# Second biases of a mixture-of-experts layer added through the gates, in attention's output product

## The chip, the core and the metric

The kernel runs on one core of a Trainium2 chip. Its engines work side by side and each takes its instructions in order: TensorE (PE, with weight loads shown apart as PEld), VectorE (DVE), ScalarE (ACT), GpSimd (POOL), and SyncE (SP), which here issues most of the DMAs. The metric is the device time of one execution in microseconds. The profile shows one execution on the same core.

## The reference, cut to what matters

Two layers are computed over `x` of shape (8, 512, 128), in float32. Each layer normalizes `x`, and adds an attention and a mixture of experts of the normalized rows to it. The change concerns layer 1:

```python
xn = layernorm(x)
x = x + attention1(xn) + experts1(xn)

# experts1, for each token t of the 4096
probs = softmax(xn @ gate_w.T)              # 8 experts
topk_probs, topk_idx = top_k(probs, 2)
hidden  = relu(xn @ w1[e] + b1[e])          # 128 -> 512
all_out = hidden @ w2[e] + b2[e]            # 512 -> 128
y = sum over the two experts e of topk_probs * all_out[e]

# attention1: the last product of each batch row
out = (gl * local + gr * remote) @ w_out
```

The second bias of an expert is a row of 128 numbers. What a token gets of all of them is the sum over its two experts of gate times `b2[e]`, which is also the product of the token's row of eight gates (six of them zero) with the 8x128 matrix `b2`.

## The kernel before, in words

**Order.** The kernel doesn't issue its instructions as it is written. A `Recorder` keeps every operation of every stage, with its engine, the tiles it reads and writes, and an estimated duration, and then a list scheduler writes out one order for all five engines (`order`). Each operation has a rank, which is spread evenly over the interval that the table `PLAN` gives to its stage: "layer0", "attention1" and "output" have an interval for each of the eight batch rows, "route" and "experts1" one for each of three groups. Among the operations that can start, the one with the earliest estimated start goes first, then the lower rank; none may run more than 60 units of rank ahead of the oldest that is left. Buffers of a tag in SBUF are given out in the order of rank, and an operation that opens a PSUM tile also claims the SBUF tiles that the later users of it open. Since all recorded instructions are issued from one helper line, the profile puts them under L389, and they are told apart by the names of their tiles. The scatters are at L1371, the loads of the experts' weights at L1336 and L1340, and the loads of the second bias at L1344.

**Fill products.** Where the estimate leaves PE idle for at least 0.6 units ahead of a fresh PSUM bank, `_fill` (L362) puts products of a tile of bfloat16 zeros there. Their results are thrown away.

**Layer 0** (`layer0`, eight times) ends with the new `x1`, the normalized rows in DRAM (`x_rows`), their transpose `x2p`, and the logits of layer 1's router. Inside it the experts' gates go through a transpose and an ACT copy (`gate_rows`: PSUM tile `gp`, SBUF tile `gT` of 8x512), are stored to DRAM and come back as broadcasts `gbc`.

**Routing** (`route`, for groups of 2, 3 and 3 batch rows). Two one-hot tiles `pick` hold the token's first and second expert, `gw` the two gates. Prefix sums over PE products give every pair of token and expert a place in a list ordered by expert, in tiles of 128 places, each tile of one expert. The outcome is `row_i` and `token_i`, the rows to scatter to and to gather from, and `own_i`, each tile's expert. There are 23, 31 and 31 tiles, 85 in all.

**Experts** (`experts1`). For a tile: SP reads the expert's number and loads its `w1` and `w2` (256 KB each) and its second bias, one row of 128 broadcast to 128 partitions (64 KB). POOL gathers the tokens' rows. PE transposes them and makes four products into `hp`; ACT adds the first bias and takes relu (four instructions, `ht`); PE makes four accumulated products into `yp`. Then DVE adds the second bias while it moves the tile out of PSUM (`ys`), and POOL scatters `ys` to `y_rows`:

```python
ys = work.tile([P, C], F32, tag="ys", name=f"ys{nm}_{j - 1}", bufs=YS)
nc.vector.tensor_add(ys, yp[:, :C], b2)
scatter(j - 1, ys)
```

**Attention** (`attention1`, eight times) computes a remote and a local part. The remote part is in `aT`. The local part ends with products into the PSUM tile `pv`; DVE forms `loc` from it, POOL adds `loc` to `aT`, PE makes four products of `aT` with `wo1` into the bank `fp`, and DVE adds `fp` to `x1`. `aT` and `loc` have one buffer each.

**Output** (`output`, eight times) loads the two rows per token from `y_rows`, and DVE adds gate times row to `x1` in eight instructions; then `x1` is stored.

Of the kernel before, what the change touches and what calls it, by code (L numbers as in the profile page):

```python
# [10 lines left out]
F32 = mybir.dt.float32  # L11
# [3 lines left out]
ALU = mybir.AluOpType  # L15
# [4 lines left out]
P = 128  # L20
B, N, C = 8, 512, 128
H, D = 16, 8
NT = N // P
E = 8
# [10 lines left out]
GROUP_OF = [(h, i) for h, n in enumerate(GROUPS) for i in range(n)]  # L35
# [400 lines left out]
def two_layers_kernel(  # L436
# [14 lines left out]
    nc = Recorder(tc.nc)  # L451
# [18 lines left out]
    def load(dst, src, queue=nc.sync):  # L470

        queue.dma_start(dst, src)
        landing[0] += 4e-6 * int(np.prod(list(dst.shape))) / 0.25
        nc.ops[-1].delay = max(2.0, landing[0] - 0.5 * len(nc.ops))
# [30 lines left out]
    we_sb = const.tile([P, E, C], F32, name="we_sb")  # L505
    load(we_sb, expert_w, nc.scalar)

    ro_sb = const.tile([P, C], F32, name="ro_sb")
    for half in (slice(0, LC), slice(LC, P)):
        load(ro_sb[half], r_out_w)  # L510
# [71 lines left out]
    def mm(o, lhsT, rhs, start=True, stop=True):  # L582
        nc.tensor.matmul(o, lhsT, rhs, start=start, stop=stop)

    def bank(name, parts=P):
        t = ps.tile([parts, 512], F32, tag="bank", name=name)
        nc.banks[t[:].tensor.name] = t[:]
        return t
# [106 lines left out]
    def gate_rows(g, name, tile):  # L695

        gp = bank(f"gp{name}")
        for t in range(NT):
            nc.tensor.transpose(gp[:E, t * P : (t + 1) * P], g[:, t, :], ident)
        gT = tile(keep, [E, N], "gT", f"gT{name}")  # L700
        nc.scalar.copy(gT, gp[:E])
        return gT
# [11 lines left out]
    for h, n in enumerate(GROUPS):  # L714
# [1 line left out]
        rows = 2 * max(GROUPS) * N + _tiles(n) * P  # L716
        y_rows.append(tc.nc.dram_tensor(f"y_rows_{h}", [rows, C], F32, kind="Internal").ap())
        logits.append(keep.tile([P, n * NT, E], F32, tag=f"logits{h}", name=f"logits_{h}", bufs=1))
    places = {}


    OTHER = {
# [200 lines left out]
    def attention1(b):  # L923

        nm = f"_{b}"
# [214 lines left out]
        nc.vector.scalar_tensor_tensor(loc, gsb[:, 0, :], 1.0, pv, ALU.add, ALU.mult)  # L1140
        nc.gpsimd.tensor_tensor(aT, aT, loc, ALU.add)
        yield
        fp = bank("fp" + nm)
        for t in range(NT):
            ts = slice(t * P, (t + 1) * P)
            mm(fp[:, ts], aT[:, ts], wo1)
        xf = x1.rearrange("p t c -> p (t c)")
        nc.vector.tensor_add(xf, xf, fp)
        late[b] = x1
# [2 lines left out]
    def route(h):  # L1152


        nm = f"_{h}"
# [14 lines left out]
        nc.vector.tensor_tensor(gw[:, 1], mx2, mx, ALU.subtract)  # L1170
        nc.scalar.activation(gw[:, 1], gw[:, 1], AF.Exp, bias=zero)
        nc.vector.tensor_mul(gw[:, 1], gw[:, 1], rs)
        m = small.tile([P, GT, E], F32, tag="ex16", name="m" + nm, bufs=1)
        nc.vector.tensor_add(m, pick[:, 0], pick[:, 1])
        mf = m.rearrange("p t e -> p (t e)")
# [133 lines left out]
    def experts1(h):  # L1309

        nm = f"_{h}"
        TILES = _tiles(GROUPS[h])
        row_i, token_i, _, bias, own_i = places[h]
        ws, xgs, xts, hts, numbers = {}, {}, {}, {}, {}

        def fetch(j):

            if j % QUAD == 0:
                n = min(QUAD, TILES - j)
                number = own_i[0:1, j : j + n]  # L1320

                def load(q=j // QUAD):
                    _, numbers[q] = tc.nc.values_load_multi_w_load_instructions(
                        number, engines=(mybir.EngineType.SP,), min_val=0, max_val=E - 1,
                        skip_runtime_bounds_check_because="a count of experts, held under E on the chip",
                    )

                nc.add("SP", load, [], [number], 1.5, 0.0)
                fetch.last = nc.ops[-1]
            first = work.tile([P, FF], F32, tag="w1", name=f"w1{nm}_{j}", bufs=3)  # L1330
            second = work.tile([P, NFC, C], F32, tag="w2", name=f"w2{nm}_{j}", bufs=4)
            third = work.tile([P, C], F32, tag="b2", name=f"b2{nm}_{j}", bufs=4)

            def load_first():
                e = bass.ds(numbers[j // QUAD][j % QUAD], 1)
                tc.nc.sync.dma_start(first, w1[e].rearrange("e p f -> (e p) f"))  # L1336

            def load_second():
                e = bass.ds(numbers[j // QUAD][j % QUAD], 1)
                tc.nc.sync.dma_start(second, w2[e].rearrange("e (k p) c -> p (e k) c", p=P))  # L1340

            def load_third():
                e = bass.ds(numbers[j // QUAD][j % QUAD], 1)
                tc.nc.sync.dma_start(third, experts_b[e, 1].to_broadcast([P, C]))  # L1344

            for move, to in ((load_first, first), (load_second, second), (load_third, third)):
                nc.add("SP", move, [to], [], 0.55, 3.3)
                nc.ops[-1].follows = (fetch.last,)
            ws[j] = first, second, third

        def gather(q):
            js = range(q * QUAD, min((q + 1) * QUAD, TILES))
            if not len(js):
                return
            xg = work.tile([P, QUAD, C], F32, tag="xgt", name=f"xgt{nm}_{q}", bufs=2)
            for a, j in enumerate(js):
                nc.gpsimd.indirect_dma_start(
                    xg[:, a], None, x_rows[h],
                    bass.IndirectOffsetOnAxis(ap=token_i[:, j : j + 1], axis=0),
                )  # L1360
            xgs[q] = xg

        views = dram_disjoint_views(y_rows[h], TILES)
        scattered[h] = []

        def scatter(j, ys):

            ids = row_i[:, j : j + 1]

            def store():  # L1370
                tc.nc.gpsimd.indirect_dma_start(  # L1371
                    views[j], bass.IndirectOffsetOnAxis(ap=ids, axis=0), ys, None
                )

            nc.add("POOL", store, [], [ys, ids], 1.25, 2.4)
            scattered[h].append(nc.ops[-1])

        def turn(q):
            if q not in xgs:
                return  # L1380
            xg = xgs.pop(q)
            n = min(QUAD, TILES - q * QUAD)
            tp = bank(f"tpx{nm}_{q}")
            for a in range(n):
                nc.tensor.transpose(tp[:, a * P : (a + 1) * P], xg[:, a], ident)
            xt = work.tile([P, QUAD * P], F32, tag="xt", name=f"xt{nm}_{q}", bufs=2)
            nc.scalar.copy(xt[:, : n * P], tp[:, : n * P])
            xts[q] = xt

        for j in range(AHEAD):  # L1390
            fetch(j)
        gather(0)
        yield
        turn(0)
        gather(1)
        yield
        for j in range(TILES + 1):
            if j < TILES:
                if j + AHEAD < TILES:
                    fetch(j + AHEAD)  # L1400
                q, a = divmod(j, QUAD)
                if a == 1:
                    turn(q + 1)
                    gather(q + 2)
                hp = bank(f"hp{nm}_{j}")
                for k in range(NFC):
                    mm(
                        hp[:, k * P : (k + 1) * P], ws[j][0][:, k * P : (k + 1) * P],
                        xts[q][:, a * P : (a + 1) * P],
                    )  # L1410
                ht = work.tile([P, NFC, P], F32, tag="ht", name=f"ht{nm}_{j}", bufs=2)
                for k in range(NFC):
                    nc.scalar.activation(
                        ht[:, k], hp[:, k * P : (k + 1) * P], AF.Relu, bias=bias[:, k, j : j + 1]
                    )
                hts[j] = ht
                yield
            if j:
                ht, (_, w2k, b2) = hts.pop(j - 1), ws.pop(j - 1)
                yp = bank(f"yp{nm}_{j - 1}")  # L1420
                for k in range(NFC):
                    mm(
                        yp[:, :C], ht[:, k], w2k[:, k],
                        start=k == 0, stop=k == NFC - 1,
                    )
                ys = work.tile([P, C], F32, tag="ys", name=f"ys{nm}_{j - 1}", bufs=YS)
                nc.vector.tensor_add(ys, yp[:, :C], b2)
                scatter(j - 1, ys)
                yield

# [21 lines left out]
    def load_next(b):  # L1452
        xs[b] = load_x(b)
        if b == 1:
# [6 lines left out]
    PLAN = {  # L1461
        "load": ((0, 1), (46, 47), (92, 93), (138, 139), (184, 185), (230, 231), (276, 277)),
        "layer0": (
            (0, 1), (0, 10), (1, 39), (77, 134),
            (121, 154), (178, 309), (241, 418), (313, 760),
        ),
        "route": ((68, 100), (273, 384), (789, 901)),
        "attention1": (
            (33, 150), (148, 194), (204, 270), (284, 611),
            (549, 789), (924, 1084), (1023, 1271), (1198, 1498),  # L1470
        ),
        "experts1": ((68, 410), (427, 1006), (967, 1293)),
        "output": (
            (676, 701), (627, 663), (1181, 1203), (995, 1107),
            (1262, 1379), (1408, 1425), (1456, 1524), (2493, 2506),
        ),
    }

# [77 lines left out]
```

## Time and profile before

| | |
|---|---|
| runs, median (lowest to highest) | 643.65 us (640.91 to 647.41), 3 runs |
| the profiled execution's own time | 641.0 us |
| its span, first to last instruction | 639.1 us |
| mean granted PE clock, as a share of full speed | 0.947 |
| busy: PE, PEld | 563.8 us (88%), 465.2 us (73%) |
| busy: DVE, ACT, POOL | 476.3 us (75%), 343.9 us (54%), 402.7 us (63%) |
| DMA | 91.63 MB, mean 143 GB/s |

The busy time of an engine is the time in which at least one of its instructions ran. A group's row gives the instructions that share engine, operation and tile names: count, busy time, mean duration in ns, then the idle time of the engine just before them and who ended it. A product of float32 operands shows as two instructions, and products overlap, so the busy time of a group of products is less than count times mean. The chain of waits is followed back from the last instruction: at each step to what released it, or to the instruction ahead of it on its engine.

### The profile page before, as it was taken

To read this page: it belongs to the slowest core of one execution; us is meant where nothing else is said; L and a number is where in the kernel's file an instruction comes from. 1 tells how busy PE (TensorE), PEld (TensorE's weight loads), DVE (VectorE), ACT (ScalarE), POOL (GpSimd) and SP (SyncE) were. 2 spreads that over 40 slices of the span, in tenths; PEclk is the share of its full clock that TensorE was granted. 3 is DMA by queue.
4 is the path that set the end of the run, shared out by engine and by line. 5 is a ranking of instruction groups with operands and counts; after the bars stand their busy time and mean duration, and the time that the engine had idled before them with its cause. 6 is when DMAs were issued, how large, how long until landed. Compare 5 with 4: busy or idle time off the path is not lost.

```text
span 639.1 us, 15660 instructions
## 1 busy us (share of the span) xinstructions
PE 563.8 (88%) x5487; PEld 465.2 (73%) x5487; DVE 476.3 (75%) x1297; ACT 343.9 (54%) x950; POOL 402.7 (63%) x422
## 2 busy tenths in 40 slices
PE   9989888798899898789999799888798988999894
PEld 3478576487777687678978679878586777888852
DVE  2797899979898899997768777878437552856594
ACT  3624639354947754475774474543744347457620
POOL 3045143788678559647668768867668586787562
PEclk8999999899999999999979899798989799899986
DMA  4044135264434246247545665677457485687222
GB/s 153 19 145 137 66 102 147 53 187 123 126 98 120 64 158 148 58 140 213 150 129 164 185 188 179 155 216 211 156 179 196 129 237 141 171 238 245 60 83 67
DMA packets 106532, 91.63 MB, mean 143 GB/s; under 512 B 8940, under 2 KB 84086, under 8 KB 106454
## 3 DMA queue, kind: packets, MB, share of 16 engines
q1 hardware_dynamic: 100582, 78.41, 42.1%
q0 software_dynamic: 5440, 11.15, 6.3%
q10 hardware_dynamic: 432, 1.07, 0.5%
q8 instruction: 44, 0.72, 0.5%
q14 instruction: 34, 0.28, 0.1%
HBM read 80.70 MB, written 9.90 MB: 142 GB/s over the span
## 4 chain that ended last, share of the span: by engine, by line
PE 37%; DVE 28%; POOL 12%; issue 9%; ACT 6%; DMA 6%; SPq 0%; POOLq 0%; DVEq 0%; ACTq 0%
PE yp L389 7%; PE hp L389 6%; PE sc L389 4%; DMA gbc<-gd 3%; POOL m L389 3%; PE rp L389 3%; DVE pw L389 3%; PE pv L389 3%; DVE xg L389 2%; POOL pw L389 2%; POOL xgt L389 2%; POOL y_rows L1371 2%; DVE m L389 2%; POOL xg L389 2%; DVE x L389 2%
## 5 line engine op out<-in xcount | busy, mean ns | idle before, releaser
L389 ACT ACTIVATE ht<-hp,bias 128x128 f32<-128x128 f32 x340 | 101.4, 373 | 51.2 <-PE hp L389 34.1
L1371 POOL DMA_INDIRECT y_rows<-ys,row_i x85 | 88.1, 1036 | 48.4 <-issue 9.8
L389 POOL DMA_INDIRECT xgt<-x_rows,token_i x85 | 87.4, 1029 | 24.8 <-issue 18.6
L389 PE MATMUL yp<-w,ht 128*128 128x128 f32 x680 | 94.6, 286 | 1.9 <-issue 1.6
L389 PEld LDWEIGHTS hp<-xt,w 128*128 128x128 f32 x680 | 86.6, 198 | 12.7 <-issue 6.7
L389 PE MATMUL hp<-xt,w 128*128 128x128 f32 x680 | 94.4, 285 | 1.2 <-DVE ys L389 0.7
L389 PEld LDWEIGHTS yp<-w,ht 128*128 128x128 f32 x680 | 86.9, 199 | 7.3 <-issue 5.3
L389 PE MATMUL rp<-we_sb,xg 128*128 128x128 f32 x512 | 67.9, 281 | 6.3 <-POOL xg L389 4.7
L389 PEld LDWEIGHTS rp<-we_sb,xg 128*128 128x128 f32 x512 | 62.2, 194 | 11.9 <-POOL xg L389 7.4
L389 POOL TENSOR_TENSOR xg<-xT,gbc 128x512 f32<-128x512 f32 x32 | 42.8, 1338 | 37.3 <-DMA gbc<-gd 25.9
L389 PE MATMUL pv<-pw,vb 128*32 128x64 f32 (+1 forms) x1088 | 37.9, 226 | 15.6 <-POOL pw L389 11.5
L389 PE MATMUL sc<-kT,qe 32*128 32x64 f32 x1024 | 45.7, 296 | 6.1 <-issue 4.8
L389 PEld LDWEIGHTS pv<-pw,vb 128*32 128x32 f32 x1088 | 33.7, 117 | 23.5 <-POOL pw L389 16.5
L389 PEld LDWEIGHTS sc<-kT,qe 32*128 32x128 f32 x1024 | 40.2, 205 | 11.9 <-issue 7.5
L389 POOL TENSOR_TENSOR pw<-pt,csb 128x512 f32<-128x512 f32 x32 | 42.5, 1328 | 3.5 <-DVE pt L389 3.3
L389 POOL TENSOR_TENSOR m<-m,amx 128x512 f32<-128x512 f32 x32 | 33.8, 1065 | 14.7 <-DVE amx L389 12.8
L389 POOL TENSOR_TENSOR m<-m,ard 128x512 f32<-128x512 f32 x32 | 34.4, 1076 | 12.7 <-DVE ard L389 3.4
L389 DVE TENSOR_TENSOR ys<-yp,b 128x128 f32<-128x128 f32 x85 | 23.5, 278 | 23.6 <-PE yp L389 19.5
L389 DVE TENSOR_TENSOR pw<-pt,csb 128x512 f32<-128x512 f32 x32 | 40.6, 1268 | 0.3
L389 POOL TENSOR_TENSOR le<-le,lrd 128x128 f32<-128x128 f32 (+3 forms) x32 | 24.0, 756 | 25.3 <-DVE lrd L389 18.3
L389 DVE COPY_PREDICATED m<-csb,sc 128x256 f32<-128x256 int32 x64 | 25.3, 435 | 19.5 <-issue 7.9
L389 ACT ACTIVATE m<-m,zero_b 128x512 f32<-128x512 f32 x32 | 23.2, 724 | 29.6 <-POOL m L389 29.6
(261 smaller groups left out, 1232.6 us busy)
## 6 DMA issues: line engine op xcount, KB each, us to landing
w<-in_w_dram SPq DMA_DIRECT2D x170, 256.0 KB
gbc<-gd SPq DMA_DIRECT2D x64, 256.0 KB
b<-in_experts_b_dram SPq DMA_DIRECT2D x85, 64.0 KB
yg<-y_rows SPq DMA_DIRECT2D x16, 256.0 KB
x<-in_x_dram SPq DMA_DIRECT2D x8, 256.0 KB
x_rows<-xn SPq DMA_DIRECT2D x8, 256.0 KB
out_dram<-x SPq DMA_DIRECT2D x8, 256.0 KB
xgt<-x_rows,token_i POOLq DMA_INDIRECT x85
```

The lines of the kernel that those rows point to most:

```text
L389: r.ENGINES[name], lambda: call(*args, **kwargs), aps[:1], aps[1:], time, delay, shape
L1371: tc.nc.gpsimd.indirect_dma_start(views[j], bass.IndirectOffsetOnAxis(ap=ids, axis=0), ys, None)
```

## The change

The second bias leaves the tiles of the experts. `route` forms `gates`, for each token its gate at its two experts and zero elsewhere. At the end of `attention1` these are transposed to `gT` (8x512, in the buffer of `loc`), and four products of `gT` with the 8x128 tile `b2_sb`, loaded once, open the accumulation in `fp`, ahead of the four old products. In `experts1` the load of the second bias goes, and ACT copies the tile out of PSUM in place of DVE's addition. The table `PLAN` has other numbers throughout.

```diff
+    b2_sb = const.tile([E, C], F32, name="b2_sb")
+    load(b2_sb, experts_b[:, 1])
...
     # attention1, after aT += loc
+        h, hb = GROUP_OF[b]
+        gT = gate_rows(gates1[h][:, hb * NT : (hb + 1) * NT], "1" + nm, lambda pool, sh, tag, name: (
+            work.tile(sh, F32, tag="loc", name=name, bufs=1)
+        ))
         fp = bank("fp" + nm)
-        for t in range(NT):
-            ts = slice(t * P, (t + 1) * P)
-            mm(fp[:, ts], aT[:, ts], wo1)
+        tiles = [slice(t * P, (t + 1) * P) for t in range(NT)]
+        for ts in tiles:
+            mm(fp[:, ts], gT[:, ts], b2_sb, start=ts.start == 0, stop=False)
+        for ts in tiles:
+            mm(fp[:, ts], aT[:, ts], wo1, start=False, stop=ts.stop == N)
...
     # route, after gw
+        both = small.tile(sh, F32, tag="rpw", name="gated" + nm, bufs=1)
+        nc.vector.tensor_tensor(both, pick, gw.unsqueeze(3).to_broadcast(sh), ALU.mult)
+        gates = small.tile([P, GT, E], F32, tag="gates", name="gates" + nm)
+        nc.vector.tensor_add(gates, both[:, 0], both[:, 1])
+        gates1[h] = gates
...
     # experts1
-            third = work.tile([P, C], F32, tag="b2", name=f"b2{nm}_{j}", bufs=4)
...
-            def load_third():
-                e = bass.ds(numbers[j // QUAD][j % QUAD], 1)
-                tc.nc.sync.dma_start(third, experts_b[e, 1].to_broadcast([P, C]))
-
-            for move, to in ((load_first, first), (load_second, second), (load_third, third)):
+            for move, to in ((load_first, first), (load_second, second)):
...
-                nc.vector.tensor_add(ys, yp[:, :C], b2)
+                nc.scalar.copy(ys, yp[:, :C])
...
     PLAN = {
         "layer0": (
-            (0, 1), (0, 10), (1, 39), (77, 134),
-            (121, 154), (178, 309), (241, 418), (313, 760),
+            (0, 1), (0, 6), (3, 45), (41, 184),
+            (132, 227), (197, 282), (255, 454), (390, 826),
         ),
-        "route": ((68, 100), (273, 384), (789, 901)),
+        "route": ((26, 48), (228, 322), (801, 988)),
         "attention1": (
-            (33, 150), (148, 194), (204, 270), (284, 611),
-            (549, 789), (924, 1084), (1023, 1271), (1198, 1498),
+            (40, 86), (110, 159), (187, 257), (319, 696),
+            (596, 1011), (987, 1227), (1232, 1332), (1290, 1606),
         ),
-        "experts1": ((68, 410), (427, 1006), (967, 1293)),
+        "experts1": ((63, 364), (375, 1040), (1032, 1380)),
...
```

More of the change, by code (lines that the diff above doesn't have):

```diff
@@ L718, in two_layers_kernel @@
         logits.append(keep.tile([P, n * NT, E], F32, tag=f"logits{h}", name=f"logits_{h}", bufs=1))
-    places = {}
+    places, gates1 = {}, {}
     OTHER = {
@@ L1340, in load_second @@
                 tc.nc.sync.dma_start(second, w2[e].rearrange("e (k p) c -> p (e k) c", p=P))
-            def load_third():
-                e = bass.ds(numbers[j // QUAD][j % QUAD], 1)
-                tc.nc.sync.dma_start(third, experts_b[e, 1].to_broadcast([P, C]))
-            for move, to in ((load_first, first), (load_second, second), (load_third, third)):
+            for move, to in ((load_first, first), (load_second, second)):
                 nc.add("SP", move, [to], [], 0.55, 3.3)
                 nc.ops[-1].follows = (fetch.last,)
-            ws[j] = first, second, third
+            ws[j] = first, second
         def gather(q):
@@ L1418, in experts1 @@
             if j:
-                ht, (_, w2k, b2) = hts.pop(j - 1), ws.pop(j - 1)
+                ht, (_, w2k) = hts.pop(j - 1), ws.pop(j - 1)
                 yp = bank(f"yp{nm}_{j - 1}")
@@ L1463, in two_layers_kernel @@
         "layer0": (
-            (0, 1), (0, 10), (1, 39), (77, 134),
-            (121, 154), (178, 309), (241, 418), (313, 760),
+            (0, 1), (0, 6), (3, 45), (41, 184),
+            (132, 227), (197, 282), (255, 454), (390, 826),
         ),
-        "route": ((68, 100), (273, 384), (789, 901)),
+        "route": ((26, 48), (228, 322), (801, 988)),
         "attention1": (
-            (33, 150), (148, 194), (204, 270), (284, 611),
-            (549, 789), (924, 1084), (1023, 1271), (1198, 1498),
+            (40, 86), (110, 159), (187, 257), (319, 696),
+            (596, 1011), (987, 1227), (1232, 1332), (1290, 1606),
         ),
-        "experts1": ((68, 410), (427, 1006), (967, 1293)),
+        "experts1": ((63, 364), (375, 1040), (1032, 1380)),
         "output": (
-            (676, 701), (627, 663), (1181, 1203), (995, 1107),
-            (1262, 1379), (1408, 1425), (1456, 1524), (2493, 2506),
+            (707, 747), (602, 635), (1386, 1421), (1092, 1223),
+            (1290, 1354), (1495, 1551), (1550, 1665), (2587, 2790),
         ),
```

## The prediction

> **What bounds the kernel now.** I read the busy shares of the whole page first.
>
> ```profile
> PE 563.8 (88%) x5487; PEld 465.2 (73%) x5487; DVE 476.3 (75%) x1297; ACT 343.9 (54%) x950; POOL 402.7 (63%) x422
> ```
>
> TensorE leads, but an average over stages hides where. So I cut the span where the DVE writes `row_i` (row 114.4 us, then about 308 and 450, the three ends of `route`) and where the last expert tile is done, and asked for busy time by stage.
>
> ```profile
> 0.00:114.40 114.40, 102.43 (x675) 72.16 (x676) 89.63 (x303) 59.58 (x143) 36.50 (x56) 0.99 0.36 110
> 114.40:308.00 193.60, 172.78 (x1814) 143.59 (x1813) 171.36 (x484) 114.03 (x301) 136.33 (x134) 0.98 0.44 125
> 308.00:450.00 142.00, 127.37 (x1332) 114.71 (x1330) 107.88 (x268) 78.87 (x232) 105.60 (x106) 0.93 0.61 177
> 450.00:608.00 158.00, 140.91 (x1479) 122.81 (x1478) 85.93 (x202) 88.05 (x269) 111.41 (x116) 0.93 0.60 173
> 608.00:639.10 31.10, 20.33 (x202) 11.90 (x199) 21.49 (x47) 3.35 (x7) 12.84 (x11) 0.77 0.27 77
> ```
>
> The columns are the stretch, its length, busy us of PE, PEld, DVE, ACT, POOL, clock, DMA share, GB/s. Call the stages A to D and the tail. In A the kernel is latency bound, and 19 us of PE's busy time in the first 128 us are the fill products on `zeros`. In B PE and DVE are both 89% busy. In C and D PE is 90% and 89% busy, while DVE falls to 76% and 54%. So the additions that this change takes from DVE lie mostly where DVE has slack, and the products it gives to PE lie where PE has little. In the chain of waits PE holds 37%, DVE 28%, POOL 12%, issue 9%, ACT 6%: the limit passes from engine to engine, and PE is the commonest holder.
>
> The tail shows in the chain as a purely serial end:
>
> ```profile
> 626.19 1.93 PE pv L389 x36
> 628.12 3.10 PE fp L362 x7
> 631.22 1.44 PE fp L389 x8
> 632.66 0.02 issue
> 632.68 0.70 DVE x L389
> ```
>
> The seven fill products put ahead of `fp` last longer than the wait that they cover: `aT` is ready at 630.2 us, the first `fp` product runs at 631.0.
>
> **The change, part by part.** The rows used:
>
> ```profile
> L389 DVE TENSOR_TENSOR ys<-yp,b 128x128 f32<-128x128 f32 x85 | 23.5, 278 | 23.6 <-PE yp L389 19.5 <-PE tpx L389 1.4 <-PE hp L389 1.2
> L389 ACT COPY pT<-tpu 128x128 f32<-128x128 f32 x8 | 2.1, 268 | 5.3 <-PE tpu L389 3.0 <-PE hp L389 1.6 <-PE yp L389 0.7
> L389 PE MATMUL fp<-wo,aT 128*128 128x128 f32 x64 | 9.5, 295 | 4.7 <-POOL aT L389 4.7
> L389 PE MATMUL gp<-csb,g 128*8 128x128 f32 x32 | 5.6, 288 | 1.7 <-issue 0.8 <-ACT gsb L389 0.5 <-DVE g L389 0.4
> L389 ACT COPY gT<-gp 8x512 f32<-8x512 f32 x8 | 4.6, 571 | 7.9 <-PE gp L389 7.8 <-issue 0.2
> L389 PE MATMUL lv<-ro_sb,lat 64*128 64x128 f32 x64 | 5.7, 297 | 3.9 <-DVE lat L389 3.6 <-PE sl L389 0.4
> ```
>
> 1. *The eviction moves.* DVE loses 85 additions, 23.5 us: by stage tables of `ys`, 4.0 before 288 us, 19.5 after. ACT gains 85 PSUM copies of 128 columns; the row of that form is `pT`, 268 ns, so 22.8 us, and ACT goes from 344 to 367. The latency to the scatter stays (278 against 268). The copy waits for `yp` in ACT's queue, as the addition did in DVE's (19.5 us). Behind it stand `ht` of the next tile, the `m` and `pT` copies: what PE needs next. ACT already waits 34.1 us on `hp`, so it is usually ahead of PE, and I cost the wait at nothing; if the cover goes, each badly placed copy costs up to the 0.27 us it lasts, some 5 us over the tiles at the outside.
>
> 2. *The gates' products.* Per batch 4 transposes to 8 rows, one ACT copy of 8x512, and 4 products of `b2_sb` ahead of the 4 old ones. Transposes: 32 at 5.6/32, 5.6 us. Copies: 8 x 571 ns, 4.6 us of ACT. For the products no row has 8 rows of contraction. The nearest is `fp` (same bank, same columns): 9.5 us for the 64 recorded instructions. The lower end is `lv`, 64 rows, 5.7 us; but its products alternate between two halves of the rows and overlap, and these all use the same eight. A guess that work shrinks with the rows would give 9.5 x 8/128 = 0.6 us. The Trainium skill (TensorE: Matmul & The Clock Gate, "Why this matters for your kernels") speaks against that: a single product over 32 rows takes as long as one over 128, and only concurrent row groups gain. No run here shows it for 8 rows; I take 9.5. PE gains 15 us, one eighth of it in the tail.
>
> 3. *Does PE have room for 15 us?* The Trainium skill (Trainium Kernel Development and Optimization, "Best Practices") says to judge the distance to the limit by the busy share of the weight loads and not of the products. By that, PE stands at 73%, C and D at 81% and 78%, and the 13 us outside the tail would vanish in gaps. By the products' rows C and D have 10 to 11% idle, most of it in pieces of under 1 us before an instruction of PE's own ("issue"), which other work can't enter; then 13 us of work cost 13 to 14.5. I take the products, nearer to the second, because waits on other engines are a small part of PE's idle time there.
>
> 4. *Route.* Each of three gets a product like `rpw` (346 ns) and a half-size addition: about 0.6 us each, 2 us of DVE, before `m` and so on the way to the first expert tile.
>
> 5. *Loads.* 85 broadcasts of 64 KB go, 5.6 of 91.6 MB, and 85 issues of SP with their waits:
>
> ```profile
> SPq L1340 <- PE yp L389: 62.9, 31, 9.9
> SPq L1336 <- PE hp L389: 45.6, 21, 8.4
> SPq L1344 <- DVE ys L389: 13.4, 13, 3.9
> ```
>
> L1344 is the issue of this load. Behind it in SP's queue stand the next tile's `w1` and `w2` and the gates' broadcasts. But SP mostly waits for PE to free the weights' buffers, and PE waited for weights 0.9 us in all; once, at 559 us, a late weight load is in the chain with 6.2 us. So the gain is 0 to 6 us; I take 1. The one new load, 8 rows at the start, stands behind `experts_row` in SP's queue and costs the next loads one issue, about 0.5 us; they are not on the first chain.
>
> 6. *The order.* All of `PLAN` is new, so the order matters as much as the operations. I weighed each instruction in both orders by its row (PE 0.27 us for a product of 128 columns, 0.15 a transpose; DVE by the means of its forms). Such sums exceed busy time by a tenth, since neighbours overlap; below they are brought down by 0.9. A: DVE +3.5 before `row_i_0`, PE the same. B: PE -9, DVE -21. C: PE +18, DVE +5. D: PE 0. So layer 0's and attention's DVE work leaves the stage where DVE binds and lands where `ys` made room; PE's work goes with it, into the stage where PE is 90% busy. Costs: A +2 (DVE is 78% busy). B between -9 (PE decides) and -21 (DVE decides), both being 89% busy: middle, -15. C +18/0.9 = +20 if PE is full, less some 3 for waits on DVE that go: +17. D -1 for the loads.
>
> 7. *The tail.* `gT` takes the buffer of `loc` (tag `loc`, one buffer), so its copy can start only when POOL has added `loc` into `aT`; the order puts the eighth batch's transposes behind seven fill products, two more fills behind those, then the gates' products, then the old ones. From 631.2 us on: transposes about 0.8 us at the lowered clock (0.60 for the four at 601 us, and 1.44 against 1.06 us for four products), copy with its handing over 0.8, products of the gates as long as the old, 1.44. Together +3 us, all on the path. In the other batches this chain lies beside expert tiles.
>
> Sum: 2 - 15 + 17 - 1 + 3 = +6 on the profiled execution's own 641.0 us (span 639.1), thus 647; the median of the runs shown is 643.65, on which +6 would be 650. I take 649, between the two.
>
> **Rivals.**
> - *PE decides everywhere* (slower). B gains only 9, C pays 20, the tail 3, A 3: +17, and with copies that hold `ht` back in ACT's queue up to +20. For it: PE is the engine with the least room from 308 us on, and PE's total grows by 15. Against: B has DVE as full as PE. Time about 659; it decides if DVE is no longer the limit in B already at -9.
> - *DVE's relief decides* (faster). B gains 21, C loses only 12 because the short waits of PE on POOL and ACT, which wait for DVE, shrink, loads give 4, the tail costs 3, A 2: -8 to -10. Time about 632. For it: DVE and POOL hold 40% of the chain. Against: DVE has 24% and 46% to spare in C and D.
> - *The edits do nothing and the new order alone decides*: this would give either sign, and is held in the two above.
>
> **The numbers.** Forecast (+1 to +12 us) 0.48, PE everywhere 0.26, DVE's relief 0.26. Within 1% (637.2 to 650.1, about what a measurement of this kernel tells from no change) lie some six tenths of the forecast and a little of the second rival: 0.31. Slower 0.43, faster 0.26. The range, from the middle of one rival to the middle of the other with a little of the rest, is 629 to 661; the forecast's own is 642 to 654.
>
> **What would show it.** `ys` copies near 268 ns on ACT; 96 more PE records on `fp` and `gp`, with 8-row products as long as 128-row ones; last `pv` to last `x` in 3 us more; `row_i` of the second route 10 to 20 us earlier, and C 15 to 20 us longer. If C does not lengthen, the faster rival is right; if `row_i` comes no earlier, the slower one.

## The result, and the profile after

The changed kernel takes 660.55 us (median of 4 runs, 659.5 to 663.57), the kernel before 643.68 us on the same chip: the ratio is 1.0266, with a 95% interval of 1.0204 to 1.0328. The profiled execution took 659.5 us, its span 657.7 us. That is 18.5 us more than the 641.0 us of before, against a forecast of 6 for that execution, and 16.9 us between the medians.

The busy shares, from the head of the page of the changed kernel:

```profile
PE 574.9 (87%) x5577; PEld 476.3 (72%) x5577; DVE 473.7 (72%) x1218; ACT 365.5 (56%) x1043; POOL 405.7 (62%) x422
```

PE has 11.1 us more to do, but it also sits idle longer: span less busy time was 639.1 - 563.8 = 75.3 us and is 657.7 - 574.9 = 82.8 us. ACT gains 21.6 us. DVE is only 2.6 us less busy though 23.5 us of additions left it: others of its instructions took longer, most of all the 64 in `output` that add gate times row (26.8 us before):

```profile
L389 DVE SCALAR_TENSOR_TENSOR x<-yg,gw,x 128x128 f32<-128x128 f32 x64 | 31.8, 526 | 5.0 <-DMA yg<-y_rows 4.9
```

POOL is 3 us busier with the same number of instructions.

The groups that were moved or added, from the groups kept apart by shape:

```profile
L389 ACT COPY ys<-yp 128x128 f32<-128x128 f32 x85 | 22.9, 270 | 29.0 <-PE yp L389 21.5 <-remote 3.3 <-PE lv L389 3.0
L389 PE MATMUL fp<-b_sb,gT 8*128 8x128 f32 x64 | 9.1, 281 | 2.2 <-ACT gT L389 1.4 <-ACT ht L389 0.8
L389 PE MATMUL fp<-wo,aT 128*128 128x128 f32 x64 | 9.4, 291 | 0.0
L389 PE MATMUL gp<-csb,gates 128*8 128x128 f32 x32 | 5.3, 291 | 0.0
```

Every new duration is as it was taken: 270 ns for the copy (268 taken), 5.3 us for the transposes (5.6), and 9.1 us for the gates' products (9.5), although they contract over 8 rows. What they add to PE's busy time is less than their sum, since they overlap with neighbours: 11.8 us by the run without them below, not 15. So the surprise is not in what the single instructions cost.

The stages, cut at the ends of the three routes and at the end of the last tile's `ys`, are in the answer of the changed kernel by stretches (stretch, length, busy us of PE, PEld, DVE, ACT, POOL, granted clock, DMA share, GB/s):

```profile
0.00:116.80 116.80, 100.92 (x725) 71.32 (x726) 89.96 (x307) 58.70 (x139) 41.50 (x57) 0.95 0.33 104
116.80:305.00 188.20, 170.07 (x1685) 144.66 (x1684) 164.22 (x419) 113.31 (x308) 123.89 (x124) 0.95 0.41 116
305.00:468.70 163.70, 145.99 (x1494) 129.62 (x1493) 113.69 (x282) 95.52 (x295) 118.80 (x119) 0.96 0.57 166
468.70:620.30 151.60, 133.50 (x1392) 115.08 (x1390) 80.30 (x160) 91.74 (x290) 104.17 (x108) 0.93 0.52 149
620.30:657.70 37.40, 24.46 (x288) 15.62 (x287) 25.49 (x54) 6.25 (x14) 17.36 (x15) 0.87 0.22 66
```

Read the length of each row first. Stage A is 2.4 us longer than before, B 5.4 us shorter (193.6 before), C 21.7 us longer (142.0 before), and from the third route to the end nothing moves (189.1 and 189.0). The loss is one stage, C, with 18.6 us more PE busy time in it than before, and too little given back by B, where PE is busy 2.7 us less and DVE 7.1.

The granted clock has a part in how this divides: it is 0.95 in B (0.98 before) and 0.96 in C (0.93 before). In a later run of the same order, without the gates' products, B had 0.98 and 185.6 us, C 0.93 and 169.0 us. So the two stages are safer read as a sum, 16.3 us more than before.

New waits stand where the change was made. From the changed kernel's list of waits (total us, times, longest):

```profile
POOL y_rows L1382 <- ACT ys L389: 40.9, 28, 6.6
...
DVE x L389 <- PE fp L389: 25.9, 6, 5.8
```

And from that of the kernel before:

```profile
POOL y_rows L1371 <- DVE ys L389: 9.6, 9, 2.1
...
DVE x L389 <- PE fp L389: 5.7, 3, 3.8
```

They are the first suspects: the evictions on ACT, and the longer chain to `fp`.

The last batch row's end, from the chain of waits of the changed kernel (start, length, what):

```profile
643.14 1.92 PE pv L389 x36
645.06 2.92 PE gp L362 x7
647.98 0.45 PE gp L389 x4
...
648.51 0.58 ACT gT L389
649.09 0.04 issue
649.13 2.26 PE fp L389 x16
651.39 0.02 issue
651.41 0.70 DVE x L389
```

The serial chain of gates is there as read from the order: seven fill products, transposes, copy (two more fill products beside it), eight recorded products in front of the old eight. From the end of `pv` to the start of DVE's addition it is 6.4 us, where it was 4.6.

### The profile page after: what moved, and what is told of

Its sections match the earlier page's. It is cut to its first block, busy times and chain, and to the rows that moved or that the text cites. A ratio compares the mean times of both kernels' runs of the same rounds, so it can differ in the third digit from the quotient of the medians.

```text
span 657.7 us, 15523 instructions
## 1 busy us (share of the span) xinstructions
PE 574.9 (87%) x5577; PEld 476.3 (72%) x5577; DVE 473.7 (72%) x1218; ACT 365.5 (56%) x1043; POOL 405.7 (62%) x422
## 4 chain that ended last, share of the span: by engine, by line
PE 37%; DVE 33%; POOL 10%; ACT 8%; issue 7%; DMA 3%; another core or an unknown queue 0%; SPq 0%; POOLq 0%; DVEq 0%; ACTq 0%
PE hp L389 6%; PE yp L389 6%; PE pv L389 3%; DVE x L389 3%; PE rp L389 3%; DVE pw L389 2%; PE fp L389 2%; POOL y_rows L1382 2%; DMA gbc<-gd 2%; ACT ht L389 2%; POOL pw L389 2%; POOL m L389 2%; DVE pt L389 2%; DVE asd L389 2%; POOL xgt L389 2%
## 5 line engine op out<-in xcount | busy, mean ns | idle before, releaser
L1382 POOL DMA_INDIRECT y_rows<-ys,row_i x85 | 91.3, 1074 | 54.1 <-ACT ys L389 40.9
L389 PE MATMUL hp<-xt,w 128*128 128x128 f32 x680 | 96.7, 289 | 5.7 <-ACT xt L389 5.6
L389 POOL DMA_INDIRECT xgt<-x_rows,token_i x85 | 83.8, 986 | 22.2 <-issue 19.4
L389 PEld LDWEIGHTS rp<-we_sb,xg 128*128 128x128 f32 x512 | 62.7, 194 | 17.7 <-issue 5.0
L389 POOL TENSOR_TENSOR pw<-pt,csb 128x512 f32<-128x512 f32 x32 | 45.7, 1429 | 4.0 <-DVE pt L389 2.9
L389 PE MATMUL pv<-pw,vb 128*32 128x64 f32 (+1 forms) x1088 | 38.1, 227 | 11.1 <-POOL pw L389 9.6
L389 PE MATMUL sc<-kT,qe 32*128 32x64 f32 x1024 | 38.9, 278 | 6.9 <-issue 4.5
L389 POOL TENSOR_TENSOR m<-m,amx 128x512 f32<-128x512 f32 x32 | 34.6, 1084 | 14.9 <-DVE amx L389 13.4
L389 PEld LDWEIGHTS sc<-kT,qe 32*128 32x128 f32 x1024 | 35.0, 189 | 12.1 <-issue 7.8
L389 ACT COPY vb<-v 32x128 f32<-32x128 f32 x128 | 37.7, 295 | 6.6 <-PE pv L389 2.8
L389 DVE TENSOR_REDUCE lmx<-sl 128x8 f32<-128x128 f32 (+3 forms) x32 | 14.3, 482 | 35.7 <-PE sl L389 23.2
L389 ACT COPY ys<-yp 128x128 f32<-128x128 f32 x85 | 22.9, 270 | 29.0 <-PE yp L389 21.5
L389 DVE TENSOR_TENSOR pw<-pt,csb 128x512 f32<-128x512 f32 x32 | 36.7, 1148 | 0.6
```

Of the source, the lines that this page charges most:

```text
L389: r.ENGINES[name], lambda: call(*args, **kwargs), aps[:1], aps[1:], time, delay, shape
L1382: tc.nc.gpsimd.indirect_dma_start(views[j], bass.IndirectOffsetOnAxis(ap=ids, axis=0), ys, None)
```

## The experiments

Three theories are told apart. Theory 1: the products that PE was given are the cost, whatever the order. Theory 2: the new table is, since it puts more PE work between the second and the third route. Theory 3, formed after the first four runs: it is the written-out order as a whole, that is how well a table fits the operations it orders, and the single edits are small. Where times from different chips are compared, the ratios to the kernel before are what counts.

**The two tables and the two sets of edits, exchanged.** Edit of the first run: the table `PLAN` of before in the changed kernel. Edit of the second: the changed kernel's table in the kernel before, and nothing else.

```diff
     # e1_edits_old_plan, against the changed kernel
-        "route": ((26, 48), (228, 322), (801, 988)),
+        "route": ((68, 100), (273, 384), (789, 901)),
     # e2_new_plan_alone, against the kernel before
-        "route": ((68, 100), (273, 384), (789, 901)),
+        "route": ((26, 48), (228, 322), (801, 988)),
     # and so for every stage
```

> All edits of the change, with the table PLAN of before. Theory 1 (the products on PE are the cost, the new intervals only deal work out among stages): 652 to 662 us, within 5 us of the changed kernel at 660.5. Theory 2 (the new order is the cost, since it gives PE more work in the stage from the second to the third route): 640 to 650 us. If it is slower than 665, the new intervals were a repair for the edits.

> The kernel before with the changed kernel's PLAN and none of its other edits. Theory 1 (products): 640 to 650 us. Theory 2 (order): 652 us or more, and the stretch between the second and third row_i stays near 160 us, as in the changed kernel (163.6), against 142.1 before.

Measured, with the kernel before at 643.3 us on that chip: 668.7 us for the edits with the old table (ratio 1.0438, 1.0372 to 1.0503), and 671.75 us for the old kernel with the new table (1.0433, 1.0378 to 1.0488). Each table is far worse with the other kernel than with its own: with the old table the edits cost 25 us, with the new one they save 11 us against leaving them out. So neither the edits nor the table has a price by itself; a table belongs to the operations that it was drawn up for. Theory 1 misses both runs, and its claim that the intervals only deal work out falls. Theory 2 has the second run right (652 or more; C even longer than near 160 us) and the first wrong (640 to 650): the old table is no repair of the changed kernel. The first run is past 665, where the expectation says that it is the other way round: the new intervals repair part of what the edits do to the old ones.

The first run loses its time in A and B (123.7 and 208.3 us, against 114.4 and 193.6 before), with C at 141.5. The second run shows where the new table puts work. Its answer by stretches:

```profile
120.60:309.00 188.40, 163.90 (x1636) 138.70 (x1635) 160.49 (x433) 106.94 (x283) 122.46 (x122) 0.95 0.42 118
309.00:478.60 169.60, 147.01 (x1485) 130.03 (x1485) 118.36 (x317) 92.04 (x270) 120.25 (x119) 0.96 0.61 175
```

B is 188 us and C 170 us, much as in the changed kernel (188 and 164), with none of its other edits. The shift from B to C comes with the table, not with the gates.

**The gates' products taken out, order kept.** The scheduler still sees these operations, so that the other instructions stand exactly as in the changed kernel; they are only not issued.

```diff
     # f1_no_products, against the changed kernel
+        nc.silent = True          # recorded, not issued
         gT = gate_rows(...)
         for ts in tiles:
             mm(fp[:, ts], gT[:, ts], b2_sb, ...)
+        nc.silent = False
         for ts in tiles:
-            mm(fp[:, ts], aT[:, ts], wo1, start=False, ...)
+            mm(fp[:, ts], aT[:, ts], wo1, start=ts.start == 0, ...)
```

> The changed kernel in its own order, with the gates' transposes, the copies to gT and the gates' products not issued, so that the second biases are missing from the output. Theory 1 (PE work of the additions is paid nearly in full): 643 to 648 us, that is 12 to 17 us less than the changed kernel, two in the tail. Rival (the cost is the eviction on ACT or the order): 655 us or more. If the gain is over 17 us, more than PE's work goes with them: the chain from aT over gT to fp holds up DVE's addition to x.

Measured: 658.99 us, ratio 1.0241 (1.0183 to 1.0299), against 1.0266 for the changed kernel. The gain of 1.6 us is inside the intervals: with both of them it is uncertain by some 5 us either way, so anything up to about 7 us fits, and the 12 to 17 us of theory 1 do not. DVE's wait for `fp` fell from 25.9 to 15.7 us. Its head of the page:

```profile
PE 563.1 (85%) x5481; PEld 467.4 (71%) x5481; DVE 474.5 (72%) x1218; ACT 361.9 (55%) x1035; POOL 406.9 (62%) x422
```

Its stages B and C:

```profile
116.80:302.40 185.60, 162.40 (x1649) 137.12 (x1648) 164.43 (x419) 111.75 (x305) 124.50 (x124) 0.98 0.42 117
302.40:471.40 169.00, 148.60 (x1482) 132.83 (x1481) 113.62 (x283) 95.38 (x294) 119.17 (x119) 0.93 0.56 161
```

PE lost 11.8 us of work, and its idle time in the span of 658.6 us rose from 82.8 to 95.5 us. What went was filled by waiting. Theory 1 falls: in this order PE's added work is not paid nearly in full. The rival's 655 us or more came in, but it names two causes, the eviction on ACT and the order.

**The eviction moved back to DVE, order kept.**

```diff
     # f2_ys_on_dve, against the changed kernel: recorded for ACT, issued on DVE at that place
-                nc.scalar.copy(ys, yp[:, :C])
+                nc.add("ACT", lambda ...: tc.nc.vector.tensor_copy(ys, yp[:, :C]), ...)
```

> The changed kernel in its own order, with the copy of yp to ys issued on DVE at the place in the order where ACT's stood. Theory 1 (products are the cost, the engine of the eviction is indifferent): 657 to 664 us. Rival (ACT's copies hold back relu and POOL's scatters, which wait 40.9 us for ys on ACT, against 9.6 us on DVE before): 645 to 655 us.

Measured: 669.7 us, ratio 1.0400 (1.0343 to 1.0456): 9 us slower, which neither theory gave. So ACT's copies are not what holds the changed kernel back; issued on DVE in an order that was drawn up for ACT, they cost more. Which wait does that was not looked into. That leaves the order as the suspect, and the same question stands in the other order.

**The edits in the order of the kernel before.** Three kernels in which the scheduler sees the operations of before, so that the order is the old one, and other instructions are issued in their places.

```diff
     # g1_old_order_no_bias_dve: no load of third, and
-                nc.vector.tensor_add(ys, yp[:, :C], b2)
+                nc.add("DVE", lambda ...: tc.nc.vector.tensor_copy(ys, yp[:, :C]), ...)
     # g2_old_order_no_bias_act: the same with
+                nc.add("DVE", lambda ...: tc.nc.scalar.copy(ys, yp[:, :C]), ...)
     # g3_old_order_all_act: g2, and in route, in the free columns of tot's bank
+            for i in range(GROUPS[h]):                       # one batch row each
+                transpose(tot[:32, (1 + i) * P : (2 + i) * P], gates of its 4 tiles)
+            scalar.copy(gT, tot[:32, P:])
     # and ahead of the old products in fp
+        matmul(fp[:], gT[:, hb * P : (hb + 1) * P], b2d, start=True, stop=False)
```

> The kernel before in its own order, without the 85 loads of second biases; DVE copies yp to ys in the place of its addition, so that the second biases are missing from the output. What the loads cost by themselves: 0 to 6 us by the prediction (638 to 644 us). Theory 3 (the written-out order is the cost, the single edits are small) expects 638 to 646.

> As the last, but the copy is issued on ACT at the place in the order where DVE's addition stood. Theory 3 (order): within 6 us of the kernel before, 637 to 650. Rival (ACT is the wrong engine for the eviction, its copies hold back relu): 652 us or more. In the changed kernel's order the copy on ACT was 9 us better than on DVE, since that order was drawn up for ACT; if the same holds here, each order favours the engine it was drawn up for, and this run is slower than the last by about as much.

> All of the change's parts in the order of the kernel before: no loads of second biases per tile, ys copied by ACT in the place of DVE's addition, the gates formed in route, and the gates' products ahead of the old ones in fp. The gates are transposed once per batch row in route, in the bank of tot, and one product of 32 rows by 512 columns per batch row with a block-diagonal tile of the biases adds them, so that attention's end gets no further copy. Theory 3 (order): 640 to 652 us, well under the changed kernel's 660.5. Theory 1 (PE's extra work and the eviction are the cost): 655 us or more.

Measured, with the kernel before at 642.7 us: 637.5 us without loads (ratio 0.9913, 0.9879 to 0.9947), 638.1 us with the copy on ACT as well (0.9929, 0.9895 to 0.9963), and 645.6 us with all parts (1.0044, 1.0008 to 1.0080). So in the old order the loads were worth 5.2 us (DVE's copy is as long as its addition, median 280 ns), the engine of the eviction 0.6 us, which is nothing, and gates with their products 7.5 us, uncertain by some 3. The first lies just under both of its ranges; the second is not the 9 us slower that its expectation allowed for; the third is theory 3's. All parts together cost 0.4%, not 2.7%. The answer of the third by stretches has the old stages back:

```profile
116.30:312.20 195.90, 177.35 (x1824) 145.89 (x1823) 172.75 (x466) 118.37 (x322) 137.35 (x134) 0.97 0.41 118
312.20:452.90 140.70, 127.30 (x1336) 111.79 (x1335) 101.56 (x243) 82.86 (x259) 106.45 (x107) 0.95 0.56 166
```

C is 140.7 us with ACT evicting (82.9 us of ACT against 78.9 before). This kernel's gates are not laid out as the changed kernel's: one product of 32 rows by 512 columns in place of four of 8 by 128, and no copy at the end of attention. The work of these products is no less, 16 instructions of 640 ns, some 10 us (an estimate from the median) against 9.1:

```profile
L1158 PE MATMUL fp<-b2d,gates x16: 587/640/1127, 167.6 to 636.2; 32*128 32x512 f32 x16
```

So the 15 us between 645.6 and 660.5 are the order and that layout together. Since taking out the gates' operations gained only 1.6 us in the new order, I put most of it down to the order; that is argued, since the layout alone was not tried there.

**One number of the scheduler.**

```diff
     # s1_ahead_55 (kernel before) and s2_after_ahead_55 (changed kernel)
-    AHEAD, TURN = 60.0, 0.15
+    AHEAD, TURN = 55.0, 0.15
```

> The kernel before with one number of the scheduler changed: operations may run 55 units of rank ahead of the oldest, not 60. The work is the same, only the order differs. Theory 3 (order): the time moves by 5 us or more, most likely up, to 648 to 670, since PLAN was drawn up with the old number. Theory 1 (work on PE decides): within 3 us of the kernel before.

Measured: 674.5 us, ratio 1.0493 (1.0443 to 1.0543), a larger move than the whole change made, and past the 648 to 670 that theory 3 held likeliest. The kernel's own operations are the same. What the scheduler adds is not: 177 fill products in place of 124, busy 49.2 us in place of 34.6 (147 and 40.1 us in the old kernel with the new table). How much of the loss these fills are was not tested. Its answer by stretches from the first route on:

```profile
120.20:331.80 211.60, 182.87 (x1787) 153.78 (x1782) 177.58 (x473) 113.92 (x298) 128.73 (x132) 0.94 0.41 119
331.80:475.70 143.90, 127.46 (x1320) 112.54 (x1319) 108.33 (x266) 76.36 (x225) 104.98 (x105) 0.93 0.60 169
```

Here C is nearly as before (143.9 us) and B is 18 us longer. So the stretched stage is not fixed: each order loses in its own place.

The same step on the changed kernel, with two more kernels, ran on another chip, on which the kernel before takes 615.9 us; only ratios are read from it.

> The changed kernel with the scheduler's 60 units set to 55, as was done to the kernel before, which went from 642.7 to 674.5 us. If the changed kernel's table is as closely fitted to its operations as the old one was to its own: 675 to 695 us. If its order is only a middling one of those that this scheduler writes: 655 to 670, either way from 660.5.

Measured: ratio 1.0579 (1.0514 to 1.0644), against the changed kernel's own 1.0266: 1.0579 / 1.0266 = 1.030, so 3.0% more; on the 660.5 us that would be 681, inside the first of the two ranges. The new table is fitted to its kernel too, if not as sharply as the old one, which lost 4.9%.

> As the run with all parts in the order of before (645.6 us), but the copy of yp to ys is on DVE, in the place of its addition. Without the biases the two engines were equal there (637.5 and 638.1); theory 3 (order) expects 643 to 648 here too. Rival (ACT's copies cost something that only shows beside the products): 641 or less.

Measured: ratio 1.0022 (0.9989 to 1.0055), no difference from the kernel before, and as good as 1.0044 with ACT. The engine of the eviction is indifferent with the products too.

> All parts of the change in the order of the kernel before, made cheap: DVE copies yp to ys in the place of its addition, the gates and the biases are split into a high and a low bfloat16 part, stacked in 96 rows, so that one bfloat16 product of 512 columns per batch row adds the second biases, and no fill products stand ahead of fp. The gates are formed behind m in route. If PE's added work in that order is what the earlier run with all parts lost against the run without biases (645.6 against 638.1 us), this one keeps most of the loads' gain: 637 to 642 us, at or under the kernel before at 642.7. If the gates' wait in route is what costs, 643 to 647.

Measured: ratio 1.0068 (1.0041 to 1.0095). The sums that its split products add are not those of the second biases, for a reason that I have not found, so its time stands only for that amount of work. With less work on PE (busy 544.2 us against 548.3) it is not faster than the run with plain products. No version here that adds all the biases beats the kernel before.

## Why the prediction was right or wrong, point by point

- *The direction* was right (slower, the likeliest of the three), and 660.5 us lies in the range, but at its upper end, where the slower rival stood: PE decides everywhere, 659. That the range held is luck: the forecast had 6 us for 18.5. The rival's terms came nearer (B -9 and C +20, measured -5.4 and +21.7), and so did its sign (`row_i` of the second route no earlier): it came 2.8 us earlier, not 10 to 20. Its reason is not borne out: it rests on PE's added work, and without the gates' products the time fell by 1.6 us.
- *Eviction* (item 1): right. 270 ns against 268, and the engine is worth 0.6 us in the old order. That the new order is 9 us worse with the copies on DVE was not foreseen.
- *Products* (item 2): durations right. The Trainium skill (TensorE: Matmul & The Clock Gate, "Why this matters for your kernels") has a single product over 32 rows take as long as one over 128; the trace agrees, and goes down to 8: 281 ns over 8 rows, 291 ns over 128.
- *PE's room* (item 3): wrong, and resting on a misreading. It says that waits on other engines are a small part of PE's idle time in C and D, and that most of it is "issue". The list of PE's waits from 288 to 608 us before has 31.8 us, of which "issue" is 6.8; the other 25 are waits on other engines. Its first three lines:

```profile
PE tpu L389 <- POOL le L389: 5.0, 3, 2.9
PE sc L389 <- issue: 4.8, 11, 1.1
PE lv L389 <- DVE lat L389: 3.6, 1, 3.6
```

So there was idle time that other work could enter, and 13 us of work were not bound to cost 13 to 14.5: in the changed kernel's order 11.8 us of busy time cost 1.6. The rule that I set aside, of the Trainium skill (Trainium Kernel Development and Optimization, "Best Practices"), to judge the distance to the limit by the weight loads' share (beside the share of peak arithmetic), states no price for added work, but pointed nearer there: 72% of the span. In the old order the gates and their products cost 7.5 us. The two prices are too uncertain to tell one order from the other.
- *Route and loads* (items 4, 5): A is 2.4 us longer (2 forecast). The loads gave 5.2 us in the old order, at the upper end of the 0 to 6 stated, not the 1 that I took. The chain of before has the late weight load of 6.2 us right behind SP's issue of a second bias; that of the run without these loads has no weight load. This may be part of the 5.2; it is not shown.
- *The order* (item 6): this is the step that failed. B was to save 15 us and saved 5.4; C was to cost 17 and cost 21.7. The two together were to cost 2 us and cost 16.3; the other stages came out 1.8 us better than their terms, which leaves the 12.5 us between 6 and 18.5. In B the terms were mis-sized: the sums of work by rows gave 9 us less PE work and 21 less DVE work, and the profile has 2.7 and 7.1 us less busy time. The step from there, that the saving lies between PE's and DVE's, held: 5.4 lies between 2.7 and 7.1. Part of the miss is the granted clock, 0.95 in place of 0.98; scaled by it, PE's 170.1 us would be 165, some 8 less than before (an estimate, as if all of it went with the clock). DVE's miss stays open. In C PE's work came as weighed (18 forecast, 18.6 measured), at a higher clock; but the 3 us of waits that were to go there did not, and PE's idle time rose by 3.1.
- *The tail* (item 7): +3 forecast, +1.8 measured from `pv` to the addition. The gates' products and the old ones took 2.26 us for 16, where 2.88 was forecast. No one forecast the clock there: in that stretch (649.1 to 651.4 us) the granted clock was 1.00, where the old products before had 0.66 (631.2 to 632.7 us).

What stays open is which waits make the new order worse. In C, PE's idle time rose only from 14.6 to 17.7 us, so the 21.7 us are mostly busy time that the table brought there, and B, with less work than before, kept 18.1 us of PE's idle time and 24.0 of DVE's (20.8 and 22.2 before). Which instruction's place does that is not shown by these runs. What they show is that the order alone, with the operations of before, moves the time by 28 to 32 us (the new table, the 55 units; the scheduler's fill products included), and that all parts of the change in the order of before move it by 2.9.

## What to carry to other kernels

Where a scheduler writes one order from a table of intervals, an edit and a new table can't be priced apart by reading: first hold the order (let the scheduler see the old operations, issue the new ones in their places), and measure the edit there. Then change one number of the scheduler alone, to learn how much an order is worth. Here that was 32 us against 2.9 for the edits, and then the edit's sign says little until the table is fitted again. A sum of durations by stage says roughly where work goes; how much busy time leaves a stage, and how much shorter the stage gets, it did not say here. And a list of waits is added up by who is waited for before a gap is called closed to other work.

## What the runs showed of the hardware that was not expected

- With PE 85 to 89% busy, removing 11.8 us of its busy time in a fixed order moved the time by 1.6 us (some 5 us either way), and adding gates and products in the other order (PE busy 572.8 against 559.2 us) moved it by 7.5 to 8.
- Two chips differ by 4% on the same kernel (642.7 and 615.9 us, medians of before). The median granted clock of these runs was 0.950 on the first and 0.971 on the second, 2.2% apart, so the clock of PE covers about half of it at most; the rest is open.
- The same 85 additions leave DVE in two orders. In the new one its busy time fell by 2.6 us, in the order of before by 14.9 (476.3 to 461.4 us, all parts with ACT); 23.5 less some 2 for the gates was expected.
